# The largest query score of a graph-attention layer: a broadcast read of one sorted row in place of two maxima and a TensorE pass

## The chip, the cores and the metric

The kernel runs on one core of a Trainium2 chip. The metric is the device time of one execution in microseconds (us). It was measured three times before the change: 2202.25, 2203.01 and 2207.36 us, median 2203.01 us.

TensorE is called PE, VectorE DVE, ScalarE ACT, GpSimd POOL, and SyncE SP; SP only issues DMAs here. "L501" is line 501 of the kernel before.

## What is computed

The input x holds 32 batches of 512 channels by 1024 nodes, in float32; adj is 512 by 512. Two layers follow each other, each with a residual and a layer norm:

```python
# layer 0: graph attention, with wm = adj
q = einsum('c,bcn->bn', wq, x);  k = einsum('c,bcn->bn', wk, x)
scores = q[:, None, :] + k[:, :, None]
scores = where(scores > 0, scores, 0.01 * scores)
att = softmax(scores, axis=-1)
agg = einsum('bcn,bmn->bcm', x, att)
x = layernorm(x + relu(einsum('oc,bcm->bom', wm, agg) + bm[None, :, None]))
# layer 1: W = adj * adj
x = layernorm(x + einsum('bnf,nm->bmf', x, W) + bias)
```

The attention is not computed as a 1024 by 1024 matrix. A score is linear in q on either side of zero. So for a node with key k the softmax needs two sums over the nodes sorted by q: those with q above -k weighted by exp(q), and those below weighted by exp(0.01 q). The exponents are taken relative to the largest q of the batch, qmax. The kernel sorts the nodes by q, builds tables of prefix sums over the sorted rows, and looks up one table row for each node.

## The kernel before

The work goes by batches; a batch passes through these steps. The short names are those in the kernel's own order lists.

- **Project** (p0 to p27, L329, PE): z = [q | wm x | k], in a scheme of seven products for four, through the PSUM banks A, B and C. ACT and DVE copy or add the results into `zrow` (128 partitions, 8 tiles of rows, 514 columns; steps k0.. and k1.., L348 and L350). Column 0 of a row is q and the last one is k. p27 is the last product and k121 the copy of its bank.
- **Largest q** (pk, mx, mr): DVE takes the maximum of q over the eight tiles (L355, one value for each partition). PE transposes that column, spread over 128, into bank C (mx, L374). DVE takes the maximum over those 128 values (L380, `qmax`) and multiplies it into two offsets (L381, `bw` = -qmax and -0.01 qmax).
- **Spread** (qb, L367, PE, 8 transposes into bank T): all 1024 q on each partition. Step ql (L386) copies it to SBUF, and step en (L360) takes the column of k aside.
- **Rank** (r0 to r7, L394, DVE): the rank of each node by counting, and its row number (L399).
- **Send** (sd0 to sd7, L406, POOL): eight indirect DMAs scatter the rows of `zrow` into a table `td` in DRAM, to their place in the order by q. Row N-1, of N = 1024, is the one with the largest q. There are two such tables, for even and odd batches.
- **Count and share** (c0 to c7, L419, ACT; sh, from L428, DVE): where each node's -k falls in the sorted order. Here qmax is used a second time.
- **Fetch** (fe, SP): eight DMAs read the sorted rows back to `zs`, two at L452 and six at L457. The text calls them F1 to F8 in their order.
- **Weigh** (wx0 and wx1, L467, ACT, with `bw` as the bias of the exponential; wb0 and wb1, L479 and L487, DVE): the weights exp(q - qmax) and exp(0.01 (q - qmax)), put into triangles. wx0 needs the blocks of F1 to F6, wx1 those of F7 and F8.
- **Tables** (t0 to t8, L501, PE; e0 to e8, L513, ACT copies them out; cp and ca, L519, POOL and ACT carry the last row of one step to the next; ts, L527, SP stores them to `td`). t8 needs what ca7 carried.
- **Pick** (pi0 to pi7, L534, POOL): eight indirect DMAs gather the table rows for each node. DVE and ACT combine them (own L549 to L551, ox1 L556, scale L573, gain L578).
- **The rest of layer 0** turns the result back (u, L587, PE), adds the residual (ad, L594, DVE), and normalizes it (L602 to L619; nb, L618, is a tiny ACT operation with one column). T1 to T4 (L643, DVE) prepare the next product.
- **Layer 1**: the bias as seeds in PSUM (sA and sB, L649, PE), the product with W (m0 to m13, L666, PE), the copies out (L689), the statistics, the apply (av, L719, ACT) and the store (L724, SP).

No scheduler decides the order. Three lists of step names are written out by hand: BEGIN for the first batches, SLOT for one turn of the steady part, and END. The loop runs SLOT for s = 1 to 28; a step with role r works on batch s + r. So a slot mixes up to five batches: while PE projects batch s + 2, the tables of batch s + 1 are built and layer 1 of batch s runs. Each engine takes its instructions in the order of the list. In SLOT the last piece before the fetch reads

```
p26 ca6 pk ad3 sq2 t7 p27 e7 ld2 mx cp7 ts7 k121 qb mr ca7 rt2 en ts4 y1 t8 r0 sA ...
```

fe is the last step of SLOT, and wx0 comes early in the next turn:

```
av3 p10 gb0 k011 p11 x13 p12 oa1 k022 p9 ox1 av0 no1 p14 gb3 sc7 k012 p15 wx0 wb0 t0 ...
```

Of the kernel before, what the change touches and what calls it, by code (L numbers as in the profile page):

```python
# [8 lines left out]
F32 = mybir.dt.float32  # L9
# [14 lines left out]
def gat_gcn_resnorm_kernel(  # L24
# [32 lines left out]
    small = ctx.enter_context(tc.tile_pool(name="small", bufs=3))  # L57
# [5 lines left out]
    ident = const.tile([P, P], F32, name="ident")  # L63
# [23 lines left out]
    for half in range(2):  # L87
        p0 = half * G
        nc.gpsimd.affine_select(
            out=tri[p0 : p0 + G, 0, :], in_=tri[p0 : p0 + G, 0, :], pattern=[[-2, G]],  # L90
# [3 lines left out]
            out=tri[p0 : p0 + G, 1, :], in_=tri[p0 : p0 + G, 1, :], pattern=[[2, G]],  # L94
# [3 lines left out]
    for row, i in ((0, 0), (G, 1)):  # L98
# [8 lines left out]
    nel = const.tile([P, 2], F32, name="nel")  # L107
# [5 lines left out]
        out=first, in_=first, pattern=[[-1, 2 * N - P]], compare_op=ALU.is_ge,  # L113
# [3 lines left out]
    zrow = const.tile([P, NT, ZW], F32, name="zrow")  # L117
# [45 lines left out]
    def bank(tag, shape, name):  # L163
        return ps.tile(shape, F32, name=name, tag=tag)
# [81 lines left out]
    bws = {}  # L246
# [2 lines left out]
    singles = {}  # L249
    tops = {}  # L250
    kcs = {}
    mxs = {}
    qmaxs = {}
    qs = {}
    tps = {}
# [93 lines left out]
        else:  # L349
            nc.scalar.copy(to, of)  # L350

    def peak(b):

        tops[b] = small.tile([P, 1], F32, name=f"q8_{b}", tag="q8")
        nc.vector.tensor_reduce(tops[b], zrow[:, :, 0], AX.X, ALU.max)  # L355

    def ends(b):

        kcs[b] = small.tile([P, NT], F32, name=f"kc_{b}", tag="kc")
        nc.vector.tensor_copy(kcs[b], zrow[:, :, C + 1])  # L360
        nc.vector.memset(zrow[:, :, C + 1], 1.0)

    def spread(b):

        qb = qbs[b] = bank("T" if b > 1 else "B", [P, N], f"qb_{b}")
        for nt in range(NT):
            nc.tensor.transpose(  # L367
                qb[:, nt * P : (nt + 1) * P], zrow[:, nt, 0:1].to_broadcast([P, P]), ident
            )

    def widen(b):

        mx = mxs[b] = bank("C", [P, N], f"mx_{b}")
        nc.tensor.transpose(mx[:, 0:P], tops.pop(b).to_broadcast([P, P]), ident)  # L374

    def highest(b):

        qmax = qmaxs[b] = small.tile([P, 1], F32, name=f"qmax_{b}", tag="qmax")
        bws[b] = small.tile([P, 2], F32, name=f"bw_{b}", tag="bw")
        nc.vector.tensor_reduce(qmax, mxs.pop(b)[:, 0:P], AX.X, ALU.max)  # L380
        nc.vector.tensor_scalar(bws[b], nel, qmax, None, ALU.mult)  # L381
# [63 lines left out]
    def fetch(b):  # L445

        zd = tdb[b % 2].rearrange("(s u) c -> s u c", u=3)
        full = zd[0 : (NB - 1) * R, 0, :].rearrange("(j q p) c -> q p j c", q=2, p=RH)
        for half in range(2):
            r = (NB - 1) * R + half * RH  # L450
            n = min(RH, N - r)
            nc.sync.dma_start(  # L452
                out=zs[half * G + 1 : half * G + 1 + n, NB - 1, 0:ZW], in_=zd[r : r + n, 0, :]
            )
        for j0, j1 in ((0, 2), (NB - 2, NB - 1), (2, NB - 2)):
            for half in range(2):
                nc.sync.dma_start(  # L457
                    out=zs[half * G + 1 : half * G + 1 + RH, j0:j1, 0:ZW],
                    in_=full[half, :, j0:j1, :],
                )  # L460

    some_blocks = (((NB - 2, NB), (0, 2)), ((0, NB - 2), (2, NB)))

    def weigh_exp(b, part):

        for i, (j0, j1) in enumerate(some_blocks[part]):
            nc.scalar.activation(  # L467
                weights(b)[:, i, j0:j1], zs[:, j0:j1, 0], AF.Exp,
                bias=bws[b][:, i : i + 1], scale=el[:, i : i + 1],
            )  # L470
# [150 lines left out]
    y1, y2 = yall[:, 0 : CT // 2], yall[:, CT // 2 : CT]  # L621
# [130 lines left out]
    def also(role, name, f, *at):  # L752
        steps[name] = role, f, at
# [91 lines left out]
    @0 wv wt1 wt0 wt2 wr2 wr1 wr0 wk x01 wt3 wl0 wl2 x02 wr3 wl1 p2 wd0 wd1 p3 x11 p4 x12 k0p1 wl3  # L845
    p0 x13 wd2 p6 x14 p7 wd3 x03 p5 k0u2 x04 p11 k0p5 @1 x01 @0 qw0 p10 p8 p1 @1 x03 @0 p9 k022 p15
    k012 p14 p17 k021 p16 p18 k1p5 @1 x11 @0 p19 @1 x02 @0 qw1 p20 k1p1 p22 p23 p21 k1u2 @1 x12 @0
    qw2 p25 @1 x04 @0 p24 k112 k011 k122 qb p26 ql p27 r0 p13 k121 r1 p12 k111 r2 en pk sd1 r3 mx @1
    p2 @0 sd0 r4 @1 p5 @0 sd3 r5 @1 p3 @0 mr sd4 r6 @1 p4 p0 @0 sd5 r7 @1 k0p1 p1 @0 sd2 @1 p7 k011
    p6 @0 sd6 @1 x14 @2 x01 @1 p12 k0u2 @0 sd7 sb0 @1 p13 p10 k0p5 p8 p9 x13 p11 k012 @2 x02 @1 p16  # L850
    @0 fe @1 k022 p17 @0 sb1 @1 p14 k1p5 p15 @0 sb2 @1 p21 k021 p19 @0 c0 @1 p18 p20 k1p1 @0 c1 @1
    k111 p22 p23 @0 wx0 wb0 t0 @2 x11 @1 k1u2 @2 x12 @1 p25 @2 x03 @0 e0 @1 p24 k112 @0 ca0 ts0 cp0
    c2 t1 @1 k122 @0 wx1 @1 qb @0 wb1 e1 @1 p27 @0 ts1 @1 ql @0 cp1 @1 pk @0 c3 @1 p26 r0 @2 p4 @1
    k121 r1 @0 c4 @1 en @0 ca1 t2 @1 r4 @0 c5 @1 sd1 r5 @2 p5 @0 e2 ca2 @1 mx @0 ts2 cp2 @1 mr @0 c6
    @1 sd4 @0 t3 @1 r2 @2 p2 @1 sd0 r3 @0 e3 ca3 ts3 cp3 @1 r6 @0 t4 @2 p1 @1 sd5 r7 @0 e4 ca4 cp4
    @1 sd3 @0 t5 @2 p3 @1 sd7 @0 e5 ts5 @2 k0p1 @0 cp5 ca5 @1 sd2 @0 t6 @2 p0 @0 e6 @2 k0p5 @0 cp6
    ts6 @2 k011 @0 ca6 @1 sd6 @0 t7 @2 x13 x14 p6 @0 e7 @2 p7 @0 ca7 cp7 ts7 t8 ts4 @2 k0u2 p11 @0
    e8 c7 @2 p10 @0 ts8 @1 fe @0 sh @2 k022 x04 p14 @0 qw3 pi0 @2 p15 p9 @1 wx0 wb0 @2 k021 @1 c0 @2
    p18 @1 t0 c1 @2 p19 @1 c2 @2 p8 @1 e0 ca0 cp0 ts0 @2 k012 @1 c3 @0 pi2 @2 k1p1 @0 pi1 @2 p22 @0
    pi3 @2 p23 @0 pi7 @2 p17 @0 pi5 @2 k1u2 p16 @1 c4 @0 pi6 @1 t1 @2 k1p5 @1 wx1 @0 pi4 @2 p24 @1  # L860
    wb1 c5 @2 p20 p12 p25 p21 p13 @0 oa0 ox0 sx no0 @2 k122 @0 sc0 @2 k112 @1 e1 @2 p27 @0 ga0 sc2
    @1 ts1 ca1 cp1 @0 sc1 gb0 @1 t2 @0 ga1 gb1 @1 e2 @0 sc3 @2 k111 @1 cp2 ca2 @0 ga2 @1 t3 @0 ga3
    gb3 @2 p26 @0 oa1 @1 e3 @0 ox1 @1 cp3 @0 no1 gb2 sc4 sc5 ga4 sc6 ga5 @1 ca3 @0 ga6 sc7 @1 t4 @0
    gb5 @1 c6 @0 ga7 gb4 gb7 @1 e4 @0 gb6 u0 @1 ca4 ts4 @2 k121 @1 cp4 ts3 c7 @0 ad0 @1 t5 ts2 @0 u1
    @1 sh e5 @0 sq0 u2 @1 cp5 @0 ad1 @1 ca5 t6 @0 rt0 @3 ld0 @2 en @0 ad2 sq1 @2 pk @0 u3 @1 e6 @3
    ld1 @2 mx @1 ca6 cp6 @0 sB @2 mr @0 sq2 rt1 ad3 @1 t7 @0 qw5 @3 ld2 @1 e7 @0 sA @1 ts6 @0 rt2 y0
    @2 qb @1 ts5 cp7 ca7 @2 r0 @1 ts7 t8 @0 sq3 @2 r1 @1 e8 @0 rt3 y1 m1 @1 ts8 @2 r2 sd1 @3 ld3 @2
    ql r3 sd0 @0 y2 m0 @2 r4 sd2 @0 y3 m7 qw4 @2 c0 @1 pi3 @0 T1 m6 @2 c1 r5 @1 pi2 @0 rdp1 m2 @1
    pi1 @0 T2 @2 c2 r6 @1 pi0 @0 m5 @2 c3 @0 T3 m4 T4 @3 x01 @0 m3 @2 r7 @0 rdu2 rd11 m9 @2 sd7 @0
# [5 lines left out]
    @28 st1 @31 p0 @29 ga2 @31 p4 @29 ga0 @31 p2 @28 st3 @31 p1 @29 ga3 @31 p3 @28 ro3 @29 gb0 @31  # L875
    p5 x11 k0p1 @29 gb2 @31 p6 k0p5 @28 st0 @31 p7 p8 @28 sf3 @29 ga1 @31 k0u2 @28 ro0 @31 x13 p10
    k011 p11 @28 sf0 @29 gb1 @28 av0 @31 p9 @29 oa1 @31 k022 @29 ox1 @28 av3 @31 p13 @29 no1 @31 p14
    @28 st2 @29 sc6 @30 wx0 @31 p15 @29 sc7 @30 wb0 @28 ro2 @30 t0 @31 k021 @29 sc4 @28 ro1 sf2 @31
    x12 p18 @29 ga6 @30 e0 @31 p19 @30 ca0 @31 k012 @30 ts0 cp0 @29 gb3 @30 t1 @31 k1p1 @29 ga7 sc5
    @31 p16 @29 gb7 @30 e1 @31 p12 @28 sf1 @30 wx1 cp1 ts1 ca1 @31 p17 @30 wb1 @28 so3 av1 @30 t2  # L880
    @29 ga4 ga5 @31 p23 @30 e2 sh @31 p22 k1p5 @30 cp2 @31 k111 @30 ca2 t3 @29 gb4 @31 k1u2 @29 gb6
    @31 p25 @30 e3 @29 gb5 @30 ca3 @29 u0 @30 cp3 @28 av2 @30 t4 @29 ad0 @28 so2 @31 p24 @30 e4 @31
    x14 @30 ca4 @29 u1 @30 ts4 cp4 @31 k122 @29 sq0 @30 ts2 t5 @29 ad1 @28 so0 @31 p20 @30 e5 ca5
    @29 u2 @30 cp5 @29 sq1 @30 t6 @29 ad2 @31 p21 @30 e6 ca6 @29 u3 @30 cp6 ts6 @31 k112 @29 sq2 @30
    ts3 @31 pk @30 t7 @29 ad3 @28 so1 @31 p27 @30 ts5 e7 ca7 @31 mx @30 cp7 ts7 @31 qb mr @29 rt0
    @30 t8 @31 ql r0 @29 rt1 @31 p26 @30 e8 @31 r1 @29 sB @30 ts8 @31 k121 @29 y0 @31 en @29 sA @31
# [79 lines left out]
```

## Time and profile before

| | |
|---|---|
| three runs | 2202.25, 2203.01, 2207.36 us |
| profiled execution | 2203.48 us, of which the span of the trace is 2201.8 us |
| PE busy (matmul) | 2109.1 us, 96% of the span |
| DVE, ACT, POOL busy | 1776.1, 1653.9, 986.5 us (81%, 75%, 45%) |
| DMA | 548.84 MB, 249 GB/s on average |
| DMA packets | 178768, of which 27020 are under 512 bytes |

Busy times are sums over instructions and leave out the issuing of DMAs. In a group's row the number before the comma is the busy time of all its instructions, the number after it the mean of one in nanoseconds, and the part behind the second bar is the time that the engine stood idle just before them and what ended it. In the timeline a bracket gives that idle time for one instruction. In the chain of waits, each row is a piece of the path that was followed back from the last instruction; "issue" is time in which an engine waited for nothing that the profile shows.

### The profile page before, as it was taken

What the parts mean: (1) busy time and instruction counts of PE and PEld (TensorE: products, weight loads), DVE (VectorE), ACT (ScalarE), POOL (GpSimd) and SP (SyncE); (2) the same over time, 40 slices, a digit from 0 to 9 for tenths busy, and PEclk for the clock granted to TensorE, in tenths of its full rate; (3) what the DMA queues carried; (4) which work ended last, traced back from release to release, by engine and by line L of the source; (5) the groups of instructions that cost most, each with busy time, mean ns of one, the idle gap of its engine ahead of it and who ended that gap; (6) DMA issues with size and microseconds to landing.
All of it is one profiled execution on the core that took longest, in us unless ns stands there. A gap on an engine that the chain in (4) does not pass through costs nothing.

```text
span 2201.8 us, 35460 instructions
## 1 busy us (share of the span) xinstructions
PE 2109.1 (96%) x11697; PEld 1235.6 (56%) x11697; DVE 1776.1 (81%) x3576; ACT 1653.9 (75%) x2758; POOL 986.5 (45%) x1291
## 2 busy tenths in 40 slices
PE   7879999999999999999999999999999999999877
PEld 5446555566555566555566555556555556655433
DVE  7568888888888888888888888788888888888666
ACT  1577777887777887777887777888777788777765
POOL 1344455443455444445443445444445544445442
PEclk9989999999999999999999999999999999999998
DMA  7568888777888778888877889878888877888762
GB/s 249 162 224 255 263 272 280 260 236 244 263 257 280 251 240 256 262 260 280 259 244 239 270 255 282 264 244 245 263 256 279 278 247 238 260 264 270 220 206 96
DMA packets 178768, 548.84 MB, mean 249 GB/s; under 512 B 27020, under 2 KB 27032, under 8 KB 178584
## 3 DMA queue, kind: packets, MB, share of 16 engines
q1 hardware_dynamic: 121216, 277.05, 43.8%
q0 software_dynamic: 57344, 269.52, 34.4%
q8 instruction: 93, 1.52, 0.3%
q14 instruction: 91, 0.75, 0.1%
q10 hardware_dynamic: 24, 0.01, 0.0%
HBM read 338.17 MB, written 208.30 MB: 248 GB/s over the span
## 4 chain that ended last, share of the span: by engine, by line
PE 73%; ACT 8%; DMA 5%; issue 4%; DVE 4%; POOL 4%; SPq 1%; POOLq 0%; DVEq 0%; ACTq 0%
PE zp_A L329 17%; PE oA L666 15%; PE tp L501 12%; PE zp_B L329 7%; PE oB L666 7%; PE op L587 5%; PE zp_C L329 4%; PE oC L666 4%; DMA zs<-td 3%; ACT rows L573 1%; ACT y L619 1%; DMA td<-zrow,ranki 1%; ACT v L689 1%; POOL zs L519 1%; PE qb L367 1%
## 5 line engine op out<-in xcount | busy, mean ns | idle before, releaser
L578 DVE SCALAR_TENSOR_TENSOR rows<-rows,ra 128x512 f32<-128x512 f32 x512 | 365.7, 738 | 19.5 <-ACT rows L573 15.7
L501 PE MATMUL tp<-zs,lq 128*64 128x257 f32 x2304 | 338.3, 394 | 27.3 <-POOL zs L519 16.6
L406 POOL DMA_INDIRECT td<-zrow,ranki x256 | 268.3, 1048 | 213.7 <-DVE idx L430 80.2
L666 PE MATMUL oA<-y,adj_sb 128*128 128x512 f32 x768 | 352.2, 601 | 9.8 <-ACT y L619 5.9
L534 POOL DMA_INDIRECT rows<-td,idx x256 | 297.2, 1161 | 90.2 <-issue 68.7
L394 DVE SCALAR_TENSOR_TENSOR junk<-qb,zrow,first 128x1024 int8<-128x1024 f32 x240 | 307.0, 1279 | 10.9 <-PE qb L367 4.0
L519 POOL COPY zs<-ts 1x513 f32<-1x513 f32 x128 | 92.0, 719 | 477.9 <-ACT ts L513 477.7
L329 PE MATMUL zp_A<-wb,x 128*64 128x257 f32 (+1 forms) x1536 | 280.3, 388 | 13.9 <-ACT v L689 6.5
L419 ACT ACTIVATE junk<-lq,kc 128x1024 int8<-128x1024 f32 x240 | 274.5, 1144 | 2.0
L594 DVE SCALAR_TENSOR_TENSOR y<-op,nbm,x 128x1024 f32<-128x1024 f32 x128 | 163.8, 1282 | 128.8 <-PE op L587 128.6
L666 PEld LDWEIGHTS oA<-y,adj_sb 128*128 128x128 f32 x768 | 146.5, 192 | 189.0 <-issue 139.5
L501 PEld LDWEIGHTS tp<-zs,lq 128*64 128x64 f32 x2304 | 171.1, 137 | 135.1 <-POOL zs L519 37.0
L573 ACT ACTIVATE rows<-rows,ra 128x512 f32<-128x512 f32 x256 | 180.0, 718 | 80.0 <-DVE ra L566 78.4
L329 PEld LDWEIGHTS zp_A<-wb,x 128*64 128x64 f32 (+1 forms) x1536 | 178.6, 155 | 77.4 <-ACT v L689 17.8
L350 ACT COPY zrow<-zp_A 128x514 f32<-128x514 f32 x192 | 112.7, 587 | 143.6 <-PE zp_A L329 129.8
L519 POOL COPY zs<-zs 1x513 f32<-1x513 f32 x128 | 79.0, 617 | 253.3 <-ACT zs L513 253.3
L619 ACT ACTIVATE y<-y,nb,r 128x1024 f32<-128x1024 f32 x128 | 158.8, 1241 | 4.3
L695 DVE BATCH_NORM_STATS2 st<-v 128x6 f32<-128x512 f32 x240 | 151.8, 674 | 0.0
L603 ACT ACTIVATE x<-y,nm 128x1024 f32<-128x1024 f32 x128 | 147.2, 1150 | 4.2
L719 ACT ACTIVATE v<-v,nb,rs 128x1024 f32<-128x1024 f32 x120 | 148.1, 1234 | 2.3 <-DVE nb L711 1.4
L587 PE MATMUL op<-ident,rows 128*128 128x128 f32 x1024 | 141.5, 283 | 4.2 <-DVE rows L578 2.0
L587 PEld LDWEIGHTS op<-ident,rows 128*128 128x128 f32 x1024 | 114.9, 143 | 46.0 <-issue 24.6
(162 smaller groups left out, 3802.6 us busy)
## 6 DMA issues: line engine op xcount, KB each, us to landing
x<-in_x_dram SPq DMA_DIRECT2D x128, 512.0 KB, 4.5
out_dram<-v SPq DMA_DIRECT2D x120, 512.0 KB, 2.9
zs<-td SPq DMA_DIRECT2D x64, 602.3 KB, 9.5
td<-zs SPq DMA_DIRECT2D x288, 120.2 KB, 4.3
td<-ts SPq DMA_DIRECT2D x224, 120.2 KB, 2.0
zs<-td SPq DMA_DIRECT2D x64, 240.9 KB, 6.9
zs<-td SPq DMA_DIRECT2D x96, 120.5 KB, 7.2
td<-zs SPq DMA_DIRECT2D x8, 514.0 KB, 7.6
```

The source lines that it names most:

```text
L329: nc.tensor.matmul(zp[n : n + wide, m, 0:CE], side(b, g, a)[:, c, m * P + n : m * P + n + wide], wb[:, w, c, :], start=first and c == 0, s ...
L394: nc.vector.scalar_tensor_tensor(junk(b)[:, 0:N], qbs[b], zrow[:, nt, 0:1], first[:, o : o + N], ALU.subtract, ALU.is_lt, accum_out=rank[: ...
L406: sc = nc.gpsimd.indirect_dma_start(out=td[:, :], out_offset=bass.IndirectOffsetOnAxis(ap=ranki[:, nt : nt + 1], axis=0), in_=zrow[:, nt, ...
L419: nc.scalar.activation(junk(b)[:, N : 2 * N], qs[b], AF.Sign, bias=kcs[b][:, nt : nt + 1], accum_out=signs(b)[:, nt : nt + 1],)
L501: nc.tensor.matmul(tp[i * G : (i + 1) * G, h, 0:CE], lw[:, ks[i], :], zs[:, j, 1 + h * CE : 1 + (h + 1) * CE], start=True, stop=True,)
L519: copy(zs[row : row + 1, to, 1:ZW], ts[row : row + 1, 0 : ZW - 1])
L534: nc.gpsimd.indirect_dma_start(out=rows[:, mt, :], out_offset=None, in_=tdb[b % 2].rearrange("(s u) c -> s (u c)", u=3), in_offset=bass.In ...
L573: nc.scalar.activation(u, u, AF.Copy, scale=ratios(b)[:, k, 1:2])
L578: nc.vector.scalar_tensor_tensor(u, rg[:, k, i, 1 : C + 1], ratios(b)[:, k, i : i + 1], u, ALU.mult, ALU.add)
L587: nc.tensor.transpose(op[:, mt * P : (mt + 1) * P], rg[:, mt, 1, 1 + ot * P : 1 + (ot + 1) * P], ident)
L619: nc.scalar.activation(yall[:, ot], yall[:, ot], AF.Identity, bias=nb, scale=r)
L666: nc.tensor.matmul(o[:, m, :], quarters[w][:, a, m * P : (m + 1) * P], part(b, y)[:, a, :], start=fresh and a == 0, stop=a == CT // 2 - 1, ...
```

## The change

The steps pk, mx and mr go, with the functions `peak`, `widen` and `highest`. The fetch begins with a ninth DMA, `top`: element 0 of the last sorted row of the DRAM table, read to all 128 partitions, is `qmax`. It is issued by SP ahead of F1 to F8. A new step bw multiplies qmax into the two offsets, on ACT. In SLOT it stands between p9 and ox1; in BEGIN (batches 0 and 1) and END (batches 30 and 31) it stands directly before wx0. The step share still reads qmax.

```diff
-    def peak(b):
-        tops[b] = small.tile([P, 1], F32, name=f"q8_{b}", tag="q8")
-        nc.vector.tensor_reduce(tops[b], zrow[:, :, 0], AX.X, ALU.max)
...
-    def widen(b):
-        mx = mxs[b] = bank("C", [P, N], f"mx_{b}")
-        nc.tensor.transpose(mx[:, 0:P], tops.pop(b).to_broadcast([P, P]), ident)
-
-    def highest(b):
-        qmax = qmaxs[b] = small.tile([P, 1], F32, name=f"qmax_{b}", tag="qmax")
-        bws[b] = small.tile([P, 2], F32, name=f"bw_{b}", tag="bw")
-        nc.vector.tensor_reduce(qmax, mxs.pop(b)[:, 0:P], AX.X, ALU.max)
-        nc.vector.tensor_scalar(bws[b], nel, qmax, None, ALU.mult)
...
     def fetch(b):
         zd = tdb[b % 2].rearrange("(s u) c -> s u c", u=3)
+        top = qmaxs[b] = small.tile([P, 1], F32, name=f"qmax_{b}", tag="qmax")
+        nc.sync.dma_start(out=top, in_=zd[N - 1, 0, 0:1].partition_broadcast(P))
...
+    def offsets(b):
+        bws[b] = small.tile([P, 2], F32, name=f"bw_{b}", tag="bw")
+        nc.scalar.activation(bws[b], nel, AF.Copy, scale=qmaxs[b])
...
-    sq1 rt0 t6 ad2 p25 ld1 rt1 e6 y0 u3 ts6 k122 cp6 k112 p26 ca6 pk ad3 sq2 t7 p27 e7 ld2 mx cp7
-    ts7 k121 qb mr ca7 rt2 en ts4 y1 t8 r0 sA e8 r1 sB sq3 ts8 m0 sh sd0 ql ld3 T1 m1 c0 sd1 r2 m3
+    sq1 rt0 t6 ad2 p25 ld1 rt1 e6 y0 u3 ts6 k122 cp6 k112 p26 ca6 ad3 sq2 t7 p27 e7 ld2 cp7
+    ts7 k121 qb ca7 rt2 en ts4 y1 t8 r0 sA e8 r1 sB sq3 ts8 m0 sh sd0 ql ld3 T1 m1 c0 sd1 r2 m3
...
-    sf0 ga1 av3 p10 gb0 k011 p11 x13 p12 oa1 k022 p9 ox1 av0 no1 p14 gb3 sc7 k012 p15 wx0 wb0 t0 x11
+    sf0 ga1 av3 p10 gb0 k011 p11 x13 p12 oa1 k022 p9 bw ox1 av0 no1 p14 gb3 sc7 k012 p15 wx0 wb0 t0 x11
```

More of the change, by code (lines that the diff above doesn't have):

```diff
@@ L251, in gat_gcn_resnorm_kernel @@
     kcs = {}
-    mxs = {}
     qmaxs = {}
@@ L762, in gat_gcn_resnorm_kernel @@
     for name, f in (
-        ("pk", peak), ("qb", spread), ("mx", widen), ("mr", highest), ("ql", line), ("en", ends),
+        ("qb", spread), ("ql", line), ("en", ends),
         ("fe", fetch),
@@ L774, in gat_gcn_resnorm_kernel @@
         also(0, f"gb{nt}", gain, nt, 0)
+    also(1, "bw", offsets)
     also(1, "sh", share)
@@ L847, in gat_gcn_resnorm_kernel @@
     k012 p14 p17 k021 p16 p18 k1p5 @1 x11 @0 p19 @1 x02 @0 qw1 p20 k1p1 p22 p23 p21 k1u2 @1 x12 @0
-    qw2 p25 @1 x04 @0 p24 k112 k011 k122 qb p26 ql p27 r0 p13 k121 r1 p12 k111 r2 en pk sd1 r3 mx @1
-    p2 @0 sd0 r4 @1 p5 @0 sd3 r5 @1 p3 @0 mr sd4 r6 @1 p4 p0 @0 sd5 r7 @1 k0p1 p1 @0 sd2 @1 p7 k011
+    qw2 p25 @1 x04 @0 p24 k112 k011 k122 qb p26 ql p27 r0 p13 k121 r1 p12 k111 r2 en sd1 r3 @1
+    p2 @0 sd0 r4 @1 p5 @0 sd3 r5 @1 p3 @0 sd4 r6 @1 p4 p0 @0 sd5 r7 @1 k0p1 p1 @0 sd2 @1 p7 k011
     p6 @0 sd6 @1 x14 @2 x01 @1 p12 k0u2 @0 sd7 sb0 @1 p13 p10 k0p5 p8 p9 x13 p11 k012 @2 x02 @1 p16
     @0 fe @1 k022 p17 @0 sb1 @1 p14 k1p5 p15 @0 sb2 @1 p21 k021 p19 @0 c0 @1 p18 p20 k1p1 @0 c1 @1
-    k111 p22 p23 @0 wx0 wb0 t0 @2 x11 @1 k1u2 @2 x12 @1 p25 @2 x03 @0 e0 @1 p24 k112 @0 ca0 ts0 cp0
-    c2 t1 @1 k122 @0 wx1 @1 qb @0 wb1 e1 @1 p27 @0 ts1 @1 ql @0 cp1 @1 pk @0 c3 @1 p26 r0 @2 p4 @1
-    k121 r1 @0 c4 @1 en @0 ca1 t2 @1 r4 @0 c5 @1 sd1 r5 @2 p5 @0 e2 ca2 @1 mx @0 ts2 cp2 @1 mr @0 c6
+    k111 p22 p23 @0 bw wx0 wb0 t0 @2 x11 @1 k1u2 @2 x12 @1 p25 @2 x03 @0 e0 @1 p24 k112 @0 ca0 ts0 cp0
+    c2 t1 @1 k122 @0 wx1 @1 qb @0 wb1 e1 @1 p27 @0 ts1 @1 ql @0 cp1 @0 c3 @1 p26 r0 @2 p4 @1
+    k121 r1 @0 c4 @1 en @0 ca1 t2 @1 r4 @0 c5 @1 sd1 r5 @2 p5 @0 e2 ca2 @0 ts2 cp2 @0 c6
     @1 sd4 @0 t3 @1 r2 @2 p2 @1 sd0 r3 @0 e3 ca3 ts3 cp3 @1 r6 @0 t4 @2 p1 @1 sd5 r7 @0 e4 ca4 cp4
@@ L857, in gat_gcn_resnorm_kernel @@
     ts6 @2 k011 @0 ca6 @1 sd6 @0 t7 @2 x13 x14 p6 @0 e7 @2 p7 @0 ca7 cp7 ts7 t8 ts4 @2 k0u2 p11 @0
-    e8 c7 @2 p10 @0 ts8 @1 fe @0 sh @2 k022 x04 p14 @0 qw3 pi0 @2 p15 p9 @1 wx0 wb0 @2 k021 @1 c0 @2
+    e8 c7 @2 p10 @0 ts8 @1 fe @0 sh @2 k022 x04 p14 @0 qw3 pi0 @2 p15 p9 @1 bw wx0 wb0 @2 k021 @1 c0 @2
     p18 @1 t0 c1 @2 p19 @1 c2 @2 p8 @1 e0 ca0 cp0 ts0 @2 k012 @1 c3 @0 pi2 @2 k1p1 @0 pi1 @2 p22 @0
@@ L864, in gat_gcn_resnorm_kernel @@
     gb5 @1 c6 @0 ga7 gb4 gb7 @1 e4 @0 gb6 u0 @1 ca4 ts4 @2 k121 @1 cp4 ts3 c7 @0 ad0 @1 t5 ts2 @0 u1
-    @1 sh e5 @0 sq0 u2 @1 cp5 @0 ad1 @1 ca5 t6 @0 rt0 @3 ld0 @2 en @0 ad2 sq1 @2 pk @0 u3 @1 e6 @3
-    ld1 @2 mx @1 ca6 cp6 @0 sB @2 mr @0 sq2 rt1 ad3 @1 t7 @0 qw5 @3 ld2 @1 e7 @0 sA @1 ts6 @0 rt2 y0
+    @1 sh e5 @0 sq0 u2 @1 cp5 @0 ad1 @1 ca5 t6 @0 rt0 @3 ld0 @2 en @0 ad2 sq1 @0 u3 @1 e6 @3
+    ld1 @1 ca6 cp6 @0 sB @0 sq2 rt1 ad3 @1 t7 @0 qw5 @3 ld2 @1 e7 @0 sA @1 ts6 @0 rt2 y0
     @2 qb @1 ts5 cp7 ca7 @2 r0 @1 ts7 t8 @0 sq3 @2 r1 @1 e8 @0 rt3 y1 m1 @1 ts8 @2 r2 sd1 @3 ld3 @2
@@ L877, in gat_gcn_resnorm_kernel @@
     k011 p11 @28 sf0 @29 gb1 @28 av0 @31 p9 @29 oa1 @31 k022 @29 ox1 @28 av3 @31 p13 @29 no1 @31 p14
-    @28 st2 @29 sc6 @30 wx0 @31 p15 @29 sc7 @30 wb0 @28 ro2 @30 t0 @31 k021 @29 sc4 @28 ro1 sf2 @31
+    @28 st2 @29 sc6 @30 bw wx0 @31 p15 @29 sc7 @30 wb0 @28 ro2 @30 t0 @31 k021 @29 sc4 @28 ro1 sf2 @31
     x12 p18 @29 ga6 @30 e0 @31 p19 @30 ca0 @31 k012 @30 ts0 cp0 @29 gb3 @30 t1 @31 k1p1 @29 ga7 sc5
@@ L884, in gat_gcn_resnorm_kernel @@
     @29 u2 @30 cp5 @29 sq1 @30 t6 @29 ad2 @31 p21 @30 e6 ca6 @29 u3 @30 cp6 ts6 @31 k112 @29 sq2 @30
-    ts3 @31 pk @30 t7 @29 ad3 @28 so1 @31 p27 @30 ts5 e7 ca7 @31 mx @30 cp7 ts7 @31 qb mr @29 rt0
+    ts3 @30 t7 @29 ad3 @28 so1 @31 p27 @30 ts5 e7 ca7 @30 cp7 ts7 @31 qb @29 rt0
     @30 t8 @31 ql r0 @29 rt1 @31 p26 @30 e8 @31 r1 @29 sB @30 ts8 @31 k121 @29 y0 @31 en @29 sA @31
@@ L890, in gat_gcn_resnorm_kernel @@
     no0 @29 m4 T3 @30 sc3 sc0 @29 rd11 @31 fe @29 rdu2 T4 @31 c4 @29 m9 @30 sc2 @31 c5 @29 m8 @31 c6
-    @29 rd22 @30 sc1 @31 c7 @29 rd12 m13 st0 @31 wx0 wb0 t0 @30 ga3 ga0 ga1 @31 e0 ca0 @29 st1 @31
+    @29 rd22 @30 sc1 @31 c7 @29 rd12 m13 st0 @31 bw wx0 wb0 t0 @30 ga3 ga0 ga1 @31 e0 ca0 @29 st1 @31
     ts0 cp0 @30 pi6 @31 t1 @30 gb1 @29 m12 @31 e1 @30 gb3 @31 ca1 ts1 cp1 wx1 @29 ro0 @31 wb1 @29
```

## The prediction

> **What bounds the kernel.** I read the page's busy times and chain first, then the groups of instructions, then one slot of the steady part, the stretch from 1036 to 1076 us, engine by engine. A slot is one turn of the SLOT list, about 65 us; there are 28, with BEGIN before and END behind. The page:
>
> ```profile
> PE 2109.1 (96%) x11697; PEld 1235.6 (56%) x11697; DVE 1776.1 (81%) x3576; ACT 1653.9 (75%) x2758; POOL 986.5 (45%) x1291
> PE 73%; ACT 8%; DMA 5%; issue 4%; DVE 4%; POOL 4%; SPq 1%; POOLq 0%; DVEq 0%; ACTq 0%
> ```
>
> PE is busy for 96% of the span, and it carries 73% of the chain. DVE time alone is therefore worth nothing; what counts is PE time on the chain and the places where PE has to wait. The groups that the change touches, and two that price it:
>
> ```profile
> L374 PE MATMUL mx<-ident,q 128*128 128x128 f32 x32 | 10.3, 323 | 2.6 <-DVE q L355 2.6
> L380 DVE TENSOR_REDUCE qmax<-mx 128x1 f32<-128x128 f32 x32 | 9.3, 290 | 42.9 <-PE mx L374 42.9
> L381 DVE TENSOR_SCALAR bw<-nel,qmax 128x2 f32<-128x2 f32 x32 | 7.5, 234 | 1.1
> L355 DVE TENSOR_REDUCE q<-zrow 128x1 f32<-128x8 f32 x32 | 5.3, 166 | 1.1
> L467 ACT ACTIVATE w<-zs,bw,el 128x2 f32<-128x2 f32 x64 | 21.1, 377 | 14.4 <-DMA zs<-td 14.4
> L618 ACT ACTIVATE nb<-nm,r 128x1 f32<-128x1 f32 x128 | 37.4, 292 | 11.3 <-POOL r L611 10.5
> ```
>
> Columns: line, engine, operation, tiles and count; then busy us and mean ns; then idle time before, with what ended it.
>
> **Removing mx (PE).** The chain shows mx on the path, with 0.25 us a slot. If that came free, 32 of them would be 8.0 us. The chain of waits, PE's timeline and ACT's timeline around it:
>
> ```profile
> 1071.82 0.87 PE zp_A L329 x8
> 1072.69 0.25 PE mx L374
> 1072.94 0.87 PE qb L367 x8
> 1073.82 1.27 PE tp L501 x7
> 1075.09 0.54 PE oA L649 x2
> ```
>
> ```profile
> 1072.09 0.57 ACT L513 COPY zs<-tp 128x514 f32<-128x514 f32 x1
> 1072.73 0.59 ACT L350 COPY zrow<-zp_A 128x514 f32<-128x514 f32 x1
> 1073.34 0.61 ACT L519 COPY zs<-zs 1x513 f32<-1x513 f32 x1
> ```
>
> The last projection ends at 1072.69. ACT then copies its bank (L350, step k121) and carries the table's last row (L519, step ca7), until 1073.95. The table's last step t8 (L501) reads what ca7 writes: its second matmul starts at 1074.01, in every slot about 0.05 us behind ca7's end, and the seeds (L649) start 1.07 us after that end. Neither copy depends on mx. Without mx, qb runs 0.25 us sooner (its bank T is free since 1072.66, L513's end), and PE then waits 0.25 us for ca7. I take 0 of the 8.0 us. What covers it is the two copies on ACT; if that cover were gone, all 8.0 us would come through.
>
> **Removing pk, mr (DVE).** DVE loses 0.166 + 0.290 + 0.234 = 0.69 us a batch, 22 us in all, and 42.9 us of idle time before L380. Its next step, r0 (L394), waits for qb on PE, and en (L360) for k121, so in the slots this gives 0. Two places in BEGIN are different, because there the ranks' chain DVE, scatter, fetch stands on the path. The first scatter of batch 0 starts at 45.59, behind L355 (45.19 to 45.34): 0.15 us. In batch 1, L355 (76.55) and L380 with L381 (82.61 to 83.09) stand among the rankings that the scatters wait for: 0.1 + 0.5 us. Together -0.75 us.
>
> **The new transfer, top.** It stands first in fetch, and the eight DMAs F1 to F8 queue behind it on SP and in the hardware queue. What waits for them is wx0 (L467, needs F1 to F6) and wx1 (needs F7, F8).
>
> ```profile
> 1036.83 0.67 SPq L452 DMA_DIRECT2D zs<-td  x2
> 1037.55 4.73 SPq L457 DMA_DIRECT2D zs<-td  x6
> 1045.48 0.21 ACT L556 ACTIVATE ac<-s 128x4 f32<-128x4 f32 x1 [1.24 <-DVE s L551]
> 1047.93 0.67 ACT L467 ACTIVATE w<-zs,bw,el 128x2 f32<-128x2 f32 x2 [0.39 <-DMA zs<-td]
> ```
>
> ```profile
> ACT w L467 <- DMA zs<-td: 16.2, 11, 6.4
> ```
>
> The bracket is the idle time before, and its cause. F6 lands 8.5 to 12.2 us after a slot's fetch begins, and ACT waits for the fetch 11 times, 16.2 us in all; where a wait is over 0.2 us, most of it comes back as PE idle (the slot at 509.70 us waits 2.23, PE 1.72). In the other 21 fetches F6 lands 0.15 to 1.56 us ahead of need. So if F6 lands D later, the cost is 11 x D, and in the other fetches what D has beyond their slack and 0.08 us of issue:
> D = 0.1 costs 1.1 us; 0.25, 2.8; 0.6, 8.3; 1.2, 23; 1.6, 35.
>
> How large is D? Top is 128 elements of 4 bytes, 8 on each of 16 engines, read from DRAM. The trace has no such read; the nearest row is the set-up of the table (L149), 4-byte writes to DRAM, in two neighbouring microseconds, 28 and 29:
>
> ```profile
> DMA packets 183, 0.29 MB, mean 294 GB/s; under 512 B 40, under 2 KB 40, under 8 KB 183
> DMA packets 456, 0.31 MB, mean 308 GB/s; under 512 B 307, under 2 KB 307, under 8 KB 456
> ```
>
> The second microsecond moved 267 more small packets, and the large ones didn't become fewer (143, then 149). A 4-byte record lasts 9 ns; 8 of them are 0.07 us an engine. 256 such elements landed 0.2 to 0.4 us behind the transfer ahead of them, which makes 0.1 to 0.2 for top's 128. The issue on SP costs 0.36 us (L149's median) and 0.05 between, so F1 to F8 are issued 0.4 later. In the slots the engines are then still at the gathers' packets, and the first fetch packet comes 1.7 us or more after its issue, so most of that is hidden. D lies between 0.1 (ring alone) and 0.6 (ring and all of the issue). It isn't below nothing: F6 is behind top in one queue. I take 0.25, nearest to the ring: **+2.8 us**, bounds 1.1 and 8.3.
>
> The Trainium skill speaks against this transfer. Its page "DMA: Bandwidth & Descriptors", section Specifications, gives 512 bytes as the least transfer for full rate, with a read-modify-write below; these are 4 bytes each. The trace's small packets, at 9 ns, do not show that price. An estimate by that rule: a packet charged as 512 bytes takes a quarter of a 2056-byte one's 149 ns, twice that with the read, 8 of them 0.6 us, D is 0.6, and the sum +7.7 us in place of the one below.
>
> **F7 and F8.** In the changed program F8 takes the semaphore that top used, so its issue waits for top's landing, at the latest that of F1, 5.3 to 7.8 us after the fetch begins, where F8 is now issued at 3.1 to 4.6. It is the last issue of the fetch, so only the table stores, 9 us later, are behind it on SP. The engines reach F7's end no sooner than 8.8 us, so F8's packets still queue in time: 0; if not, wx1, which has 0.2 to 2.5 us to spare, is late.
>
> **bw on ACT.** Two columns, about 0.29 us (L618's row). In SLOT it stands ahead of ox1 (L556), where ACT idles 1.2 us for DVE's s; F1, behind top in the queue, lands at least 0.57 us before ox1 starts. So the wait for top ends sooner and bw fits: 0. Behind bw on ACT are ox1, av0, sc7 and wx0, so a late top would hold all of them. In BEGIN and END it stands right before wx0. In batch 0 wx1's wait for F8 covers it, in batches 1 and 31 wx0's own (6.41 and 1.14 us); only batch 30 pays, with a slack of 0.31 us: **+0.2**.
>
> **Sum.** 0 + 0 - 0.75 + 2.8 + 0.2 = +2.2 us. The profiled execution took 2203.48 us (span 2201.8 and 1.7 around it), so 2205.7. That execution is 0.47 above the median of three, 2203.01, so the forecast for the median is 2205.2. A run of this kernel can be told from no change beyond 0.3%, 6.6 us: this forecast is "no change".
>
> **Rivals.**
> B, slower: small packets read from DRAM are not cheap. If each costs what one of the fetch's 2056-byte packets does (149 ns median), 8 make 1.2 us, and 1.6 with the issue: +23 to +35 us, 2226 to 2238. It decides from D of about 0.5, where the cost passes 6.6 us. For it: no such read in the trace, and 11 fetches without slack. Against: the 9 ns of the writes. The same mechanism shows at bw, if top lands later than about 8.4 us after the fetch begins.
> C, faster: mx's PE time comes through, because ca7 moves forward with it. -8.0 - 0.75 + 0.2 + 1.1 to 2.8 gives -5.8 to -7.5, 2195.5 to 2197.2. Against: k121 follows the last projection, which doesn't move.
> D, the change only trades: top lies wholly behind the gathers and D is about 0: -0.5, 2202.5, inside my range.
>
> **Chances.** The forecast (with D) 0.70, of which 0.13 is a D from 0.5 to 0.6, slower by over 0.3%; B 0.23; C 0.07, nearly all of it just beyond the bound. So slower 0.36, same 0.58, faster 0.06. The range goes from C's near end, 2197, to B's near end, 2227: it leaves out most of B and the far end of C.
>
> **What would show it.** In the profile after: qb follows the last projection directly, and a PE gap of about 0.25 us stands before t8's second matmul, released by ACT (if not, C). The wait of L467's successor for the fetch grows from 16.2 us by about 3, to 19 or 20; 30 or more means B. bw starts without a wait for top in the slots. SP shows the last fetch issue later, and wx1 doesn't wait more. I am wrong if the slots grow by more than 0.2 us each, or shrink by 0.2.

## The result and the profile after

Six runs of the changed kernel took 2206.38 to 2215.43 us, median 2213.09; six of the kernel before 2199.94 to 2207.36, median 2203.37. The ratio is 1.0039, 95% interval [1.0021, 1.0057]: slower by 0.4%, about 8.6 us. The profiled execution is the shortest of the six, 2206.38 us with a span of 2204.7: its trace is 2.9 us longer than that of before and shows only part of the loss.

The page of the changed kernel, busy times and chain:

```profile
PE 2109.3 (96%) x11633; PEld 1235.6 (56%) x11665; DVE 1760.9 (80%) x3480; ACT 1661.7 (75%) x2790; POOL 971.4 (44%) x1291
PE 66%; ACT 9%; DVE 8%; DMA 7%; issue 5%; POOL 3%; SPq 1%; DVEq 0%; POOLq 0%; ACTq 0%
```

DVE lost about 15 us and PE none, although mx is gone. The groups that answer to those shown of before (L456 is the old L467, L361 the old L367):

```profile
L456 ACT ACTIVATE w<-zs,bw,el 128x2 f32<-128x2 f32 x64 | 21.2, 379 | 12.1 <-DMA zs<-td 11.4 <-ACT bw L451 0.6
L451 ACT ACTIVATE bw<-nel,qmax 128x2 f32<-128x2 f32 x32 | 9.1, 285 | 4.8 <-DMA qmax<-td 4.7
L361 PEld LDWEIGHTS qb<-ident,zrow 128*128 128x128 f32 x256 | 27.1, 136 | 15.7 <-ACT zs L502 14.6 <-DVE zrow L347 1.1
```

The exponentials wait less for the fetch in this trace than in that of before, not more, and bw takes 285 ns of ACT. Around the removed step, the chain of waits, then ACT's row for ca7 (L508) in the same slot, then SP's timeline at the fetch:

```profile
1070.08 0.87 PE zp_A L328 x8
1070.95 0.02 issue
1070.97 1.09 PE qb L361 x8
1072.06 1.29 PE tp L490 x8
1073.35 0.32 PE oA L638
```

```profile
1071.60 0.61 ACT L508 COPY zs<-zs 1x513 f32<-1x513 f32 x1
```

```profile
1034.51 0.34 SPq L431 DMA_DIRECT2D qmax<-td  x1
1034.94 0.96 SPq L436 DMA_DIRECT2D zs<-td  x2
1035.95 6.66 SPq L441 DMA_DIRECT2D zs<-td  x6
```

qb follows the last projection at once. ca7 ends at 1072.21 and the seeds (L638) start 1.07 us later (at 1073.28 in PE's timeline), as before: mx's time did not come through. There was hardly any to come: from the last projection's end to qb's end it is 1.11 us in the slots of both traces of the changed kernel, and 1.13 to 1.23 in those of before, with mx between. For qb starts 0.05 us behind the copy that empties its bank T (L502, 14.6 of the 15.7 us of idle time in the row of L361), and mx ran beside the end of that copy. The eight fetch DMAs take SP 7.7 us here, 5.5 in the prediction's lines, since the last waits for top's semaphore.

**Where the time went.** I call the stretch from one batch's seeds to the next a slot; stretch 1 starts with batch 0's seeds. A clean one takes 65.0 us in both kernels (65.02 and 65.05). The rest of the time is in slots that are not clean. One kind is more frequent than before. Here is a slot of the changed kernel with seeds at 1204.43 us (17): POOL's, ACT's and PE's timelines.

```profile
1207.85 1.02 POOL L388 DMA_INDIRECT td<-zrow,ranki  x1 [0.31 <-issue]
1210.39 1.05 POOL L523 DMA_INDIRECT rows<-td,idx  x1 [1.52 <-DMA td<-zs]
1212.40 0.29 ACT L607 ACTIVATE nb<-nm,r 128x1 f32<-128x1 f32 x1 [0.99 <-POOL r L600]
1212.73 1.24 ACT L608 ACTIVATE y<-y,nb,r 128x1024 f32<-128x1024 f32 x1
1214.03 1.98 PE L655 MATMUL oC<-y,adj_sb 128*128 128x512 f32 x4 [0.84 <-ACT y L608]
```

And a clean one, with seeds at 1401.58 (20):

```profile
1405.00 1.01 POOL L388 DMA_INDIRECT td<-zrow,ranki  x1 [0.31 <-DMA td<-zs]
1406.32 1.06 POOL L523 DMA_INDIRECT rows<-td,idx  x1 [0.30 <-PE oA L655]
1408.78 1.24 ACT L608 ACTIVATE y<-y,nb,r 128x1024 f32<-128x1024 f32 x1
1409.32 3.60 PE L655 MATMUL oC<-y,adj_sb 128*128 128x512 f32 x8
```

In slot 17 the first pick (L523) waits 1.52 us for the last table store. Behind it on POOL are the steps that give the last normalization its scale (L599, L600). So y3, the last y (L608), starts 8.3 instead of 7.2 us after the seeds, and PE stands 0.84 us within bank C's product. I call such a slot late (y3 later than 7.6 us). Stretch 1, where y3 comes at 8.6 to 9.0 us in every kernel, isn't counted. In the trace of before 8, 9, 19, 20 and 27 are late, in that of the changed kernel 6 to 8, 16 to 18, 27 and 28. Why the store lands late shows in the DMA queues from 0.5 to 4.5 us after the seeds, late slot first, then the clean one (columns: transfers, MB, share of 16 engines):

```profile
q1 hardware_dynamic: 452, 0.80, 74.3%
q8 instruction: 1, 0.02, 1.5%
q14 instruction: 1, 0.01, 0.6%
```

```profile
q1 hardware_dynamic: 453, 0.81, 81.4%
q14 instruction: 1, 0.01, 0.5%
```

A packet of q8 is there: 16 KB of instructions, which took 0.96 us of one DMA engine, from 1.72 us after the seeds. In the clean slot the nearest one came at 7.7 us. Both have an 8 KB packet of instructions on q14; it alone doesn't make a slot late (in the first of the held kernels below, nine slots have one at 1.2 to 1.7 us and none is late). The page counts 93 packets of q8, 1.52 MB. That is PE's code: the trace of before has 23919 PE records, and at the 64 bytes that the Trainium skill gives an instruction ("Perfetto Trace Analysis", The 4-stage abstract model) they make 1.53 MB. The 16 KiB are also the block in which it says an engine's instruction memory is refilled ("Runtime: NRT & Kernel Launch", Terms); here every packet of q8 has 16384 bytes. That they delay the kernel's own transfers is for the runs below to show.

256 instructions are one transfer: the traces have 23919 PE records to 93 transfers before, 24607 to 96 and 25245 to 98 in two kernels below, 256 to 258 each time. PE runs 746 of them in a slot before the change and 744 after (some traces, the first of the changed kernel among them, lack one record a slot), so the transfers' place drifts by 22 or 24 instructions a slot, and comes round after 11 slots or so.

### The profile page after: what moved, and what is told of

Its sections match the earlier page's. It is cut to its first block, busy times and chain, and to the rows that moved or that the text cites. A ratio compares the mean times of both kernels' runs of the same rounds, so it can differ in the third digit from the quotient of the medians.

```text
span 2204.7 us, 35327 instructions
## 1 busy us (share of the span) xinstructions
PE 2109.3 (96%) x11633; PEld 1235.6 (56%) x11665; DVE 1760.9 (80%) x3480; ACT 1661.7 (75%) x2790; POOL 971.4 (44%) x1291
## 3 DMA queue, kind: packets, MB, share of 16 engines
q8 instruction: 93, 1.52, 0.3%
## 4 chain that ended last, share of the span: by engine, by line
PE 66%; ACT 9%; DVE 8%; DMA 7%; issue 5%; POOL 3%; SPq 1%; DVEq 0%; POOLq 0%; ACTq 0%
PE zp_A L328 17%; PE tp L490 11%; PE oA L655 11%; PE zp_B L328 8%; PE op L576 5%; PE oB L655 5%; PE zp_C L328 4%; DMA zs<-td 3%; PE oC L655 3%; DVE junk L376 2%; ACT y L608 2%; ACT rows L562 2%; DMA td<-zs 2%; DMA td<-zrow,ranki 1%; POOL zs L508 1%
## 5 line engine op out<-in xcount | busy, mean ns | idle before, releaser
L567 DVE SCALAR_TENSOR_TENSOR rows<-rows,ra 128x512 f32<-128x512 f32 x512 | 366.4, 740 | 17.1 <-ACT rows L562 13.9
L523 POOL DMA_INDIRECT rows<-td,idx x256 | 282.2, 1102 | 93.4 <-issue 69.6
L376 DVE SCALAR_TENSOR_TENSOR junk<-qb,zrow,first 128x1024 int8<-128x1024 f32 x240 | 307.1, 1280 | 14.6 <-PE qb L361 6.1
L508 POOL COPY zs<-ts 1x513 f32<-1x513 f32 x128 | 91.6, 716 | 476.0 <-ACT ts L502 475.8
L328 PE MATMUL zp_A<-wb,x 128*64 128x257 f32 (+1 forms) x1536 | 277.9, 387 | 13.8 <-ACT zrow L349 3.6
L508 POOL COPY zs<-zs 1x513 f32<-1x513 f32 x128 | 78.3, 612 | 256.3 <-ACT zs L502 256.3
L608 ACT ACTIVATE y<-y,nb,r 128x1024 f32<-128x1024 f32 x128 | 158.8, 1241 | 4.3
```

Source lines behind the costliest of these rows:

```text
L328: nc.tensor.matmul(zp[n : n + wide, m, 0:CE], side(b, g, a)[:, c, m * P + n : m * P + n + wide], wb[:, w, c, :], start=first and c == 0, s ...
L376: nc.vector.scalar_tensor_tensor(junk(b)[:, 0:N], qbs[b], zrow[:, nt, 0:1], first[:, o : o + N], ALU.subtract, ALU.is_lt, accum_out=rank[: ...
L508: copy(zs[row : row + 1, to, 1:ZW], ts[row : row + 1, 0 : ZW - 1])
L523: nc.gpsimd.indirect_dma_start(out=rows[:, mt, :], out_offset=None, in_=tdb[b % 2].rearrange("(s u) c -> s (u c)", u=3), in_offset=bass.In ...
L567: nc.vector.scalar_tensor_tensor(u, rg[:, k, i, 1 : C + 1], ratios(b)[:, k, i : i + 1], u, ALU.mult, ALU.add)
L608: nc.scalar.activation(yall[:, ot], yall[:, ot], AF.Identity, bias=nb, scale=r)
```

## The experiments

The expectations call the prediction's theory Q: the cost is top, ahead of F1 to F6. I is the theory of the instruction transfers; J takes the late slots for chance, and K blames the lost steps of DVE.

**The changed kernel again**, unaltered.

> The changed kernel, unaltered, for a second trace. Two theories. Q (the prediction's): top ahead of F1 to F8 makes F6 land later, so the waits of L456 for the fetch and the PE gaps behind them grow. I (instructions): the 16 KB instruction transfers of queue q8 (93 of them, 1.52 MB, about PE's code of 364 + 364 + 16 instructions a slot at 64 bytes) come at a place of the slot that drifts by 1.5 KB of code a slot; where one falls between 0.6 and 2 us after the seeds, the last table store lands after 4.0 us instead of 3.4 to 3.7, the first pick waits, step y3 is late and the product into bank C waits 0.4 to 0.8 us. The first trace had 9 such slots in 28, the trace before 5. I expects the same slots to be hit again (5 to 7, 15 to 17, 26 to 28 by the y step, a slot or so to either side), and the time at 2206 to 2215 us. Q expects waits of L456 of 17 us or more in this trace; I expects 10 to 16.

Measured: 1.0038 [1.0025, 1.0052], 2211.03 us against 2202.57. The late slots were 6 to 8, 15 to 18, 27 and 28; in the first trace 6 to 8, 16 to 18, 27 and 28. In all but the 15 a transfer of q8 starts between 0.5 and 1.7 us after the seeds. They recur, so they aren't chance. (The expectation numbers them by the y step, one lower.) The wait of L456 for the fetch was 17.1 us here, just in Q's forecast and outside I's, and 12.0 in the first trace; before the change it was 16.2 and, in a second trace, 21.8. It varies by more than what Q asks for, so it doesn't decide.

**The removal alone.**

```diff
+    level = const.tile([P, 1], F32, name="level")
+    nc.vector.memset(level, 4.0)
+    offset = const.tile([P, 2], F32, name="offset")
+    nc.vector.tensor_scalar(offset, nel, level, None, ALU.mult)
...
-        top = qmaxs[b] = small.tile([P, 1], F32, name=f"qmax_{b}", tag="qmax")
-        nc.sync.dma_start(out=top, in_=zd[N - 1, 0, 0:1].partition_broadcast(P))
+        qmaxs[b] = level
...
-        nc.scalar.activation(bws[b], nel, AF.Copy, scale=qmaxs[b])
+        bws[b] = offset
```

> Only the removal: pk, mx, mr are gone as in the changed kernel, and so are top and bw; the offset that is taken off the exponents is the constant 4.0 instead of the batch's largest q. Q expects 2203.4 - 0.75 = 2202.6 us, the changed kernel's 2213 being all due to top and bw. I expects it slower than before although it only takes work away, because PE's code has the changed kernel's length: 8 to 10 hit slots in 28, 2206 to 2213 us. If mx's PE time came through after all (rival C), 2195.

Measured: 1.0037 [1.0020, 1.0053], 2211.06 us. Work was only taken away, and the kernel lost as much as the changed one. Q falls here. The number of late slots, which I set at 8 to 10, was only 4 in its trace (8, 16, 17, 28). Of the others that were late in the changed kernel, the transfer came 2.6 and 2.2 us ahead of the seeds in 6 and 27, and 0.1 and 1.0 us behind them in 7 and 18, where y3 was later by 0.3 us at most. The four cost 4.9 us over clean slots, no more than the late slots of before. So late slots alone do not account for this kernel's time.

**The addition alone.**

```diff
+    spare = const.tile([P, 1], F32, name="spare")
...
         zd = tdb[b % 2].rearrange("(s u) c -> s u c", u=3)
+        nc.sync.dma_start(out=spare, in_=zd[N - 1, 0, 0:1].partition_broadcast(P))
```

> Only the addition: the kernel before with the transfer top first in each fetch, into a tile that nothing reads; pk, mx, mr stay and no bw. Q expects the whole of the loss here: 2203.4 + 2.8 (bounds +1.1 and +8.3), up to 2213. I expects 2203 to 2206, 5 or 6 hit slots as before, since PE's code is that of before.

Measured: 1.0006 [0.9995, 1.0016], 2203.89 us; late slots 8, 9, 19 and 20, as in the kernel before without its 27. Top is worth -1 to +3.5 us, most likely 1.3. F6 landed 9.90 us after the fetch began in the mean of 32, against 9.90 before and 9.80 and 9.94 in the changed kernel: D is 0 within 0.1.

**Turning the drift.** In the changed kernel, from batch 3 on:

```diff
-        wide = G if f"p{i}" in NARROW.split() else P
+        wide = G if f"p{i}" in (NARROW if b < 3 else NARROW + MORE).split() else P
...
+    MORE = " p0 p3 p5 p15 p21 p26"
```

> The changed kernel, where from batch 3 on the products p0, p3, p5, p15, p21 and p26 are cut into half-wide matmuls as 20 others are already: 24 more PE instructions a slot, the same work (a wide pair took 0.45 us, a narrow four the same in the trace). PE's code of a slot becomes 744 + 24 = 768 instructions, 48 KB, exactly three instruction transfers, so they should stay at their place of slot 1, where none falls near the table stores. I expects 0 to 2 hit slots, and 2213 - 8 = about 2205 us or below, 2200 at the best. Q expects no change from 2213, or more if the narrow form costs.

Measured: 1.0017 [1.0004, 1.0029], 2207.02 us. My count was wrong: a narrow product adds eight PE instructions, not four, so a slot has 792, and q8 went from 93 to 98 transfers. The drift turned round (the transfer now came earlier from slot to slot) instead of stopping, and 9 slots were late again. What was gained came otherwise: a clean slot fell from 65.02 to 64.79 us with the narrow products.

**The kernel before again**, unaltered.

> The kernel before, unaltered, for a second trace and as the null comparison: ratio 1.000 within 0.0015. Theory I (instructions) expects the slots whose y3 starts later than 7.6 us after the seeds to be the same as in its first trace (8, 9, 19, 20 and perhaps 27), with an instruction transfer of q8 between 1 and 2 us after the seeds in each. Rival J (jitter): the late slots are chance, and are others this time.

Measured: 0.9993 [0.9983, 1.0004]; late slots 8, 9, 19 and 20, a transfer of q8 at 1.4 to 1.9 us in each. J falls: these four are late in every trace of this kernel; only 27, which has no such transfer, is in one trace and not in the other.

**Holding the place, clear of the table stores.** The changed kernel:

```diff
-        wide = G if f"p{i}" in NARROW.split() else P
+        wide = G if f"p{i}" in (NARROW + more(b)).split() else P
...
+    def more(b):
+        return " p15 p21 p26" if b > 2 else " p0 p3 p5 p15 p21 p26" if b == 2 else ""
```

> The changed kernel with PE's code of a slot at 768 instructions: from batch 3 on the products p15, p21 and p26 are cut into narrow matmuls (8 more PE instructions each, as the 48 more of the run with six showed; that run went past 768 to 792 and the drift turned round). Batch 2 has six such products, which moves the place by 24 more. The same work. I expects the transfers of q8 to stand still at about 10, 41 and 55 us after the seeds, no slot with a late y3 (before: 8 or 9 of 28), and 2211 - 8 to -14: 2197 to 2203 us. J expects no change: 2211.

**Holding it on the table stores.** The same, with

```diff
+        return " p15 p21 p26" if b > 8 else ""
```

> The same three narrow products, but only from batch 9 on, when the drifting transfer of q8 has come to 1 to 2 us behind the seeds. The same work. I expects it to stay there: 18 to 23 slots of 28 with a late y3 in place of 8 or 9, each 0.7 to 1.1 us, so 2211 + 10 to +15: 2221 to 2226 us; another transfer then also stands at 36 to 37 us, beside the fetch, which can cost more. J expects 2211.

Measured: 2195.44 us, 0.9970 [0.9958, 0.9982], and 2224.24 us, 1.0096 [1.0082, 1.0111]. The waits of PE for y, of before, after, the first and the second of these:

```profile
PE oC L666 <- ACT y L619: 5.4, 7, 1.7
```

```profile
PE oC L655 <- ACT y L608: 6.8, 11, 0.8
```

```profile
PE oC L655 <- ACT y L608: 0.8, 2, 0.4
```

```profile
PE oC L655 <- ACT y L608: 22.3, 24, 1.3
```

Columns: us in total, times, longest. Held at 10 to 13 us after the seeds, the transfers made no slot late; held at 0 to 2 us, 21 of 28. From batch 9 on the two kernels run the same instructions, and 29 us lie between them; the six batches more with narrow products in the first make only about 6 x 0.24 = 1.5 of these. I holds. The first is faster than both the kernel before and the changed one.

**The kernel before, held in the same way**: from batch 2 on, and then from batch 3 on, since the first drifted back to the stores in its last slots.

```diff
+        return " p15 p21 p26" if b > 1 else ""
```

> The kernel before with the same three narrow products from batch 2 on (746 + 24 = 770 PE instructions a slot, nearly three transfers). I expects no late y3 and 2203 - 4 to -10: 2193 to 2199 us; and against the changed kernel with the same treatment a difference of 0 to 3 us, since what the removal cost was the place of the transfers. J expects 2203, and the changed kernel 8 us above it.

> The kernel before with p15, p21 and p26 narrow from batch 3 on instead of batch 2, so that the transfers start 24 instructions further from the seeds and, with 770 instructions a slot, don't drift back to them by the last slots (the first such run had three late slots, two of them the last). I expects no late y3 and 2193 to 2196: with no late slot in either, the kernel before and the changed one (2195.4) are equal within 2 us. If the removal has a cost of its own, apart from the transfers' place, this kernel is 4 to 8 us faster than the changed one held in the same way.

Measured: 0.9972 [0.9960, 0.9983], 2196.57 us, late slots 15, 27 and 28; and 0.9957 [0.9942, 0.9972], 2193.12 us, none late. This is the fastest kernel of the study.

**The removal alone, held.** As above, with the batches' choice of the changed kernel.

> Only the removal (constant 4.0 in place of the largest q, no top, no bw), with PE's code held at 768 instructions as in e6_after_lock3. The difference from that run, 2195.4, is the price of top and bw without the transfers' place in it. Theory Q2 (the prediction's term, with D = 0.25): 2195.4 - 3 = 2192.4. I, after the run with top alone (1.0006 [0.9995, 1.0016]): 2194 to 2196.

Measured: 0.9971 [0.9959, 0.9982], 2196.63 us, none late. With and without top and bw the held kernels are the same (0.9970), so top and bw cost nothing that shows.

**mx's two instructions back, and two others.** First, in the changed kernel, mx in its old places of the lists:

```diff
+    def widen(b):
+        mx = bank("C", [P, N], f"mx_{b}")
+        nc.tensor.transpose(mx[:, 0:P], zrow[:, 0, 0:1].to_broadcast([P, P]), ident)
```

> The changed kernel with a TensorE transpose in mx's old place between p27 and qb, on a column of zrow, into bank C; nothing reads it. pk and mr stay away, top and bw stay. PE's code of a slot is 746 instructions again and PE stands ahead of qb as before. Theory I1: what the removal costs is mx's place, since the code that PE's sequencer fetches ahead ends two instructions earlier at qb's wait, and the transfers of q8 fall behind the seeds in three slots of a cycle in place of two. It expects 2203 to 2205 and late y3 in slots 8, 9, 19, 20 only. I2: any two instructions would do (the drift of 22 instead of 24 a slot): the same here, and also in the next run. Rival K (the lost DVE steps pk and mr move POOL's and ACT's work): stays at 2211.

Then, in step u0:

```diff
-        for mt in range(NT):
+        for mt in ([0] if ot == 0 else []) + list(range(NT)):
```

> The changed kernel with the first transpose of step u0 (the turn of layer 0's result) done twice, the second overwriting the first with the same values: 746 PE instructions a slot, as before, but far from qb, and 0.1 us more of PE work in a slot (28 x 0.1 = 3 us at the most). I2 expects 4 or 5 late slots and 2203 to 2207; I1 and K expect 8 or 9 late slots and 2211 to 2214.

Measured: 1.0017 [1.0009, 1.0026], 2208.1 us, and 1.0040 [1.0026, 1.0053], 2211.66 us. The extra pass of the second showed in each clean slot (65.16 us instead of 65.05), 28 x 0.11 = 3 us; without that it would stand at about 2208.6. So both bring back some 3 of the 8 us and neither brings back all. Their traces show two different shares of it. With mx the edge moves. I count in PE instructions from the transfer's number times 256 back to the seeds, with the record a slot that some of these traces lack put back. Then a transfer falls behind the seeds at -207 but not at -215 in the traces of before, and at -213 but not at -227 with mx; at -235 but not at -243 in those of the changed kernel, and at -231 but not at -245 with u0's pass doubled. So with mx the edge lies where it lay before, as near as these steps tell, and with the other pair where the changed kernel has it. That speaks for I1, with a doubt: in the removal alone, whose PE code is the changed kernel's, a transfer fell behind the seeds at -235, but ahead of them at -227 and -219. With either, the transfers come round later, so that the third passage, which made slots 27 and 28 late in the changed kernel, doesn't fall on the last slots: slots 7 to 9, 19 and 20 are late by q8 with mx (and 3 and 26 without a transfer there), 6 to 8 and 18 to 20 with u0's. That speaks for I2. Neither is refuted, both missed their times of 2203 to 2207, and K is not excluded for the rest.

## Why the prediction was right or wrong

The measured median lies in the range (2197 to 2227) and the sign was right, but that was luck: the term that made the sum positive, top, shows no price, and the loss came with the removal, to which the prediction gave -0.75 us. The loss was forecast at 2.2 us and measured at 8.6. The class that came, slower by over 0.3%, had a chance of 0.36, no change 0.58.

- **mx on PE.** That PE's time isn't gained was right: a clean slot keeps its 65.0 us. The cover was another than the two copies named. The chain's 0.25 us for mx lay beside the copy that empties bank T; qb ends only 0.02 us sooner in most slots. The forecast gap of 0.25 us before t8's second matmul isn't there: from qb's end to that matmul it is 0.20 us, 0.19 before, and still it isn't C, since ca7 ends 1.26 us behind the last projection as before. The step that failed is the price: "I take 0 of the 8.0 us". The removal alone cost 8 us. It was priced by time only; that it shortens PE's code, and so moves the instruction transfers against the table stores, wasn't in the sum, and no rival had it. That PE runs up to qb's wait sooner, and fetches otherwise for it, is only argued.
- **Top.** The term of +2.8 us was mis-sized: alone, top measured 1.0006, 1.3 us, and D is 0, not 0.25. When the fetch is issued the engines are still at work on the gathers (queue q0 held 85.9% of them from 1036.83 to 1038.5 us in the trace of before), and the issue and 128 small packets go unseen. Rival B, small packets at the price of large ones, is excluded: it asked for 23 us or more. So is the estimate that the prediction made from the rule of 512 bytes, 8.3 us for top and +7.7 for the sum: the interval of top alone ends at +3.5.
- **pk and mr on DVE.** -0.75 us in BEGIN couldn't be seen: batch 0's seeds came at 151.26 and 152.04 us in two traces of before, at 150.88 and 152.71 in two after.
- **bw.** Nearly right: 285 ns, hidden in most slots. It waited for top in four slots, 2.0 us in all, which the prediction had at none (2.8 of the 4.7 us in the row of L451 are batch 1's in BEGIN, which it had); in two of these top landed 7.8 and 7.9 us after the fetch began, in the others 6.6 and 6.8.
- **F8.** Right: it is issued 4.2 to 8.1 us after the slot's fetch begins, and lands at 13.9 to 17.3 us, against 13.8 to 16.7 before.
- **Rival C** fell for the reason given against it: ca7 did not move against the last projection.

The sum by the runs: holding the place of the transfers took 2211.0 - 2195.4 = 15.6 us from the changed kernel and 2203.6 - 2193.1 = 10.5 from the one before. Of each, 27 x 0.24 = 6.5 us is the shorter clean slot with narrow products. The rest is 9.1 and 4.0 us. The late slots are of that size: 8.5 and 13.5 us over the length of clean slots in the two traces of the changed kernel (the 13.5 with another wait of 2.8 us in one of them), 5.9 and 6.1 in those of before. So about 5 of the 8 us are the place of the instruction transfers. This is a difference of four medians, and their intervals leave some 5 us to either side of it. The stretch behind the last slot fits: it is late (7.8 to 7.9 us, with a transfer of q8 at 1.2 to 1.5) in all three traces with the changed kernel's PE code, and in none of the three with that of before (7.2). What doesn't fit is the removal alone, which lost as much with 4.9 us of late slots.

Between the held kernels 2.3 us remain, 3.5 for the removal alone, and the intervals overlap. Whether the lost steps of DVE have a price of their own, whether the 8 KB instruction transfers of q14 cost something elsewhere in a slot, and where the part went that neither pair of instructions brought back, stays open. The traces can't tell: one a kernel scatters by as much (spans of 2201.8 and 2208.9 us in two of the same kernel).

## What to carry to other kernels

In this kernel, whose steady part has hardly any slack, the place of the instruction transfers made up to 29 us with the same work; a change of two instructions a turn can cost more through it than through its own time. Count the instructions of the longest queue in a turn of the loop: where they are not a multiple of a transfer's 256, the transfers drift through the turn, and some turns may pay; a few instructions more, of the same work, held them here at a place where nobody waits. Measure a removal and an addition apart before either is blamed.

## What was not expected of the hardware

- A transfer of 16 KB of instructions takes 1.1 us of one DMA engine (mean of 93). Where it meets the table stores, the last store lands 4.2 to 5.7 us after the seeds instead of 3.3 to 3.7 in most clean slots, and a slot becomes about 1.1 us longer.
- A broadcast read of 4 bytes to 128 partitions, first in a queue of eight larger reads, left those reads where they were (F6 landed at 9.80 to 9.94 us, 9.90 without).
- Cutting three more 128-wide fp32 products into 64-wide halves added 24 PE instructions and shortened a clean slot from 65.01 to 64.77 us; six did no more (64.79).
